# Last FFN product transposed and in one-pass format, causal mask in tiles of 32 rows, in a planned attention and FFN kernel

## Chip, core and metric

The kernel runs on one core of a Trainium2 chip. The metric is the device time of one execution in microseconds, the median of several runs. All of the work is one launch: inputs come from HBM, the activations stay on chip through all four layers, and the result goes back to HBM.

## What is computed

The input x has 16 sequences of 256 tokens with 128 features. Four residual layers follow each other, each on a layer-normalized input: attention a (2 heads of 64, part of each head rotated), an FFN, attention b (16 heads of 8 with a causal mask), and the same FFN with the same weights once more.

```python
x = x + attn_a(layernorm(x))
x = x + ffn(layernorm(x))
x = x + attn_b(layernorm(x))
x = x + ffn(layernorm(x))

def ffn(x):                                  # tlin(x, w, s) = (x @ w.T) * s
    h = silu(tlin(x, w1_w, w1_s)) * tlin(x, w2_w, w2_s)       # 128 -> 512
    h = gelu(tlin(h, h1_w, h1_s), approximate=False)          # 512 -> 512
    h = gelu(tlin(h, h2_w, h2_s), approximate=False)          # 512 -> 512
    return tlin(h, w3_w, w3_s)                                # 512 -> 128

# attn_b: the mask hides query positions before the key; softmax over the keys
scores = where(arange(n)[:, None] <= arange(n)[None, :], scores, -10000.0)
```

The FFN's weights hold only -1, 0 and 1; their scales stand in vectors of their own.

## The kernel before

**Tiles.** The 4,096 tokens are cut into eight batches (`NP`) of 512 tokens (`TOK`), that is two sequences. The residual of batch i stays in the SBUF tile `XR[i]`. An FFN works on transposed activations, features on the partitions and 512 tokens along the row. There are 16 FFN passes, eight with the tag `f` after attention a and eight with the tag `g` at the end.

**The planner.** The kernel's operations are not issued as they are written. Each is recorded as an `Op` with an engine, a cost in us written by hand, and a rank. `Plan.laid` then lays them out on a modelled clock, always taking on each engine one that could begin first (`WEIGH` says how much a change of table or of matmul mode counts there), and among near equals the one with the lowest value of `order_of`, from the table `ORDER` with a start and a step per batch for every stage. Each tile of a `Group` takes one of its buffers, and an operation can't be laid before one is free. The result is a fixed order on each engine. An operation given by `either` goes to whichever of two or three engines the planner takes. Every recorded instruction has the line 291 in the profile, so groups are told apart by tiles: `w` is a PSUM bank or a shared work buffer, `s` the four-bank score buffer, of which there is one (`g_scores`), `h` a hidden layer, `u` a Gelu or Silu output.

**The FFN.** The full-precision matmuls of this kernel run as two instructions each in the trace. Most FFN products avoid them: `parts` rounds an activation to the one-pass format as `hi` and keeps the remainder as `lo`, and `product` multiplies both halves with weights that are exact in that format. At the start a check on ACT (`low`) sums the bits that rounding would lose; where there are any, a second branch of the program runs, which is not run here. The first layer's two products have 128 features in, the two hidden ones 512. A hidden layer takes two buffers of `g_h` (hi and lo), of which there are four, handed out in turn. The second Gelu writes a full-precision tile of its own (`g_h2`, called `hl` in the profile; other tiles called `hl` in the code stand in shared buffers called `w`). The last product is full precision and not transposed: for each of four blocks of 128 tokens, the activation is the stationary side and `w3_sb`, 128 wide and multiplied by its scale beforehand, the moving one:

```python
        for t in range(TB):
            pe = p("PE", 0.87, "1")
            for c in range(NC):
                pe.matmul(
                    py[:, t * E : (t + 1) * E],
                    lhsT=h[:, c, t * P : (t + 1) * P],
                    rhs=w3_sb[:, c, :],
                    start=(c == 0),
                    stop=(c == NC - 1),
                )
```

The result already has tokens on the partitions, and DVE adds it to `XR[i]`.

**Attention b.** For each of 16 sequences the kernel goes twice through all scores, in four groups of four heads. First `attention_b_max` forms them with queries on the partitions: eight matmuls that each use 32 rows of the array, four at a time in its four row groups. Four matmuls of all 128 rows then add the mask, a diagonal `eye` times a tile `hide` of zeros and -3e38, and a reduction on DVE takes the maxima. Then `attention_b` forms the scores again with keys on the partitions, with the maxima subtracted by row-packed matmuls with `pick`; ACT takes the exponential and POOL clears the masked part. Both go through the one buffer `s`.

Of the kernel before, what the change touches and what calls it, by code (L numbers as in the profile page):

```python
# [11 lines left out]
F32 = mybir.dt.float32  # L12
F32R = mybir.dt.float32r
# [81 lines left out]
class Plan:  # L95
# [5 lines left out]
    WEIGH = {"ACT": 1.54, "PE": 0.00}  # L101
# [67 lines left out]
    def laid(self):  # L169
# [28 lines left out]
        for _ in range(len(self.ops)):  # L198
            best = None
            for e, ops in ready.items():  # L200
# [23 lines left out]
                if not cands:  # L224
# [5 lines left out]
                    (x for x in cands if x[0] + weigh * x[1] <= first + 0.012),  # L230
# [63 lines left out]
class _Recorder:  # L294
# [19 lines left out]
P = 128  # L314
# [27 lines left out]
    (INPUT, "a"): (-781, 18.6),  # L342
    (MAIN, "a"): (-863, 52.3),
    (NORM, "f"): (377, 0),
    (FILL, "f"): (88, 87.2),
    (INPUT, "b"): (299, 73.8),
    (MAXIMA, "b"): (-1830, 180.0),
    (MAIN, "b"): (448, 22.6),
    (NORM, "g"): (827, 180.7),
    (FILL, "g"): (423, 113.4),  # L350
}
LATER_AT = -505
# [17 lines left out]
R_BQKV, R_BO, R_OB, R_W3S, R_FREQ, R_END = 0, 384, 512, 640, 768, 769  # L370

C_BQ, C_BK, C_BV, C_W1S, C_W2S, C_H1S, C_H2S, C_END = 0, 1, 2, 3, 7, 11, 15, 19
# [3 lines left out]
def hybrid_kernel(ctx: ExitStack, tc: tile.TileContext, x, rows, cols, wa, wb, w12, h1, h2, w3, out):  # L376
# [28 lines left out]
    g_u, g_h, g_h2 = group("u", 4), group("h", 4, True), group("hl", 1)  # L405
# [15 lines left out]
    w3_sb = fixed([P, NC, E], "w3_sb")  # L421
# [16 lines left out]

    w12v, h1v, h2v = w12, h1.rearrange("(c p) o -> p c o", p=P), h2.rearrange("(c p) o -> p c o", p=P)
# [3 lines left out]
    for dst, src, lag in ((w12_sb, w12v, 8.0), (h1_sb, h1v, 10.0), (h2_sb, h2v, 14.0)):  # L443
        rounded.append(load("POOL", lag, dst, src, "weights"))
        exact.append(p.tile(work, [P, src.shape[1], DH], F32, f"w{len(exact)}", g_32 if exact else g_16))
# [5 lines left out]
    load("SP", 16.0, w3_sb, w3.rearrange("(c p) o -> p c o", p=P), "loads")  # L451
# [52 lines left out]
    for t in range(2):  # L504
# [13 lines left out]


# [7 lines left out]
    hide = fixed([P, 2 * P], "hide", BF16)  # L527
    o = p("POOL", 0.8)
    o.memset(hide[:], 0.0)
    o.affine_select(  # L530
        out=hide[:].rearrange("p (b k) -> p b k", b=2),
        in_=hide[:].rearrange("p (b k) -> p b k", b=2),
        compare_op=ALU.is_ge,
        fill=-HUGE,
        base=0,
        pattern=[[0, 2], [-1, P]],
        channel_multiplier=1,
    )
    eye = fixed([P, P], "eye", BF16)
    p("POOL", 0.3).tensor_copy(eye[:], ident[:])  # L540
# [48 lines left out]
    for c in range(NC):  # L589
        p("POOL", 0.45).tensor_tensor(w3_sb[:, c, :], w3_sb[:, c, :], rows_sb[:, R_W3S : R_W3S + E], ALU.mult)  # L590
# [13 lines left out]
    for n, w in enumerate(exact):  # L604
        k = w.tile.shape[1] * DH
        bits = w[:].rearrange("p c o -> p (c o)").bitcast(U16).rearrange("p (n b) -> p n b", b=2)[:, :, 0]
        p("ACT", 0.25 + 0.82e-3 * k).activation(
            p.tile(work, [P, 2048], mybir.dt.bfloat16, f"junk{n}", g_24)[:, 0:k], bits, AF.Copy, accum_out=low[:, n : n + 1]
        )
# [24 lines left out]

    def sb(shape, name, g, quota=None, dtype=F32):
        return p.tile(work, shape, dtype, name, g, quota)
# [11 lines left out]
    def layernorm_T(i, what, bias=None):  # L648
# [20 lines left out]
        for t in range(TB):  # L669
            by, mean = rstd[:, t : t + 1], mv[:, t, 0:1]  # L670
            p.either(
                ("DVE", 0.26, "tensor_scalar", (xh[:, t, :], XR[i][:, t, :], mean, by, ALU.subtract, ALU.mult), {}),
                ("ACT", 0.24, "activation", (xh[:, t, :], XR[i][:, t, :], AF.Identity), {"bias": shift[:, t : t + 1], "scale": by}),
            )
# [129 lines left out]
    def attention_b_inputs(i):  # L804
# [3 lines left out]
        for name, c0, bias in (("q", 0, C_BQ), ("k", P, C_BK)):  # L808
# [5 lines left out]
                ("ACT", 0.67, "activation", (hl[:, 0, :], pp[:], AF.Identity), {"bias": plus}),  # L814
                ("DVE", 0.72, "tensor_scalar", (hl[:, 0, :], pp[:], plus, None, ALU.add), {}),
            )
            p("DVE", 0.77).scalar_tensor_tensor(hl[:, 1, :], pp[:], plus, hl[:, 0, :], ALU.add, ALU.subtract)
# [24 lines left out]
    def attention_b_max(i, s, q0, k0, q1, k1, v):  # L842
# [10 lines left out]
        for g in range(4):  # L853
# [3 lines left out]
            o = p("PE", 0.28 + 0.15 + 0.42, ("4r", "1"))  # L857
# [12 lines left out]
            for a in range(4):  # L870
                o.matmul(sc[:, a, P : 3 * P], lhsT=eye[:], rhs=hide[:], start=False, stop=True, skip_group_check=True)
# [181 lines left out]
    def ffn(i, what):  # L1053
# [35 lines left out]
        for layer, (w_sb, wv, cs) in enumerate(((h1_sb, h1v, C_H1S), (h2_sb, h2v, C_H2S))):  # L1089
            h_in = h  # L1090
            h = sb([P, NC, TOK], f"h2_{n}", g_h2) if layer else hidden(1)
            phs = [bank(f"ph{layer}_{n}_{o}") for o in range(NC)]
            us = [h[:, o, :] if layer else sb([P, TOK], f"t_{n}_{o}", g_u)[:] for o in range(NC)]
            ps = [
                product(ph, w_sb, wv, slice(o * P, (o + 1) * P), *h_in, NC, [u] + ([] if layer else h), part_of=o)
# [7 lines left out]
            for o, (ph, u) in enumerate(zip(phs, us)):  # L1103
                if o > 1:
                    ps[o](0, 2 * NC)
                p("ACT", 0.59, "gelu", rank=(FIRST, what, i, 0)).activation(u, ph[:], AF.Gelu, scale=cols_sb[:, cs + o : cs + o + 1])
                if not layer:
                    parts(h, o, u)
        py = bank(f"pf_{n}")
        for t in range(TB):  # L1110
            pe = p("PE", 0.87, "1")
            for c in range(NC):
                pe.matmul(
                    py[:, t * E : (t + 1) * E],
                    lhsT=h[:, c, t * P : (t + 1) * P],
                    rhs=w3_sb[:, c, :],
                    start=(c == 0),
                    stop=(c == NC - 1),
                )
# [5 lines left out]
    g_m3 = group("m3", 2)  # L1125

# [73 lines left out]
```

## Time and profile before

| | |
|---|---|
| median of 3 runs | 787.37 us (785.58 to 787.78) |
| the profiled execution | 785.15 us |
| its span | 783.4 us |
| first and last score matmul of attention b | 187.4 and 712.8 us |
| granted TensorE clock, mean | 0.984 |
| table loads on ACT | 103, 132.1 us |

Busy time is the time in which an engine worked on an instruction; a matmul's record lasts from its start to the end of its pipeline, so records of matmuls overlap, and the busy time of a group is the union of its records. In the rows of groups the columns are the busy time of all, the mean of one in ns, and after the second bar the idle time of the engine in front of them with what ended it. In the chain's rows and the timeline's, the first number is the start and the second the duration, in us.

### The profile page before, as it was taken

The numbers are of one execution on the slowest core, as the hardware profiler recorded it, in microseconds if no ns is written. First come the engines' busy times: TensorE is split into PE (matmuls) and PEld (weight loads), VectorE is DVE, ScalarE is ACT, GpSimd is POOL, SyncE is SP. The second block draws the span as 40 slices with busy tenths as digits, with TensorE's granted clock in tenths as the row PEclk, the third lists the DMA queues.
The fourth block names the chain that finished last, engine by engine and source line by source line (L and its number), as shares of the span: only waits on it lengthen the run. The fifth ranks groups of instructions, "written<-read, shape, count | busy, mean of one in ns | idle before, by whom it ended". The sixth has DMA issues, their size and how long they took to land.

```text
span 783.4 us, 14329 instructions
## 1 busy us (share of the span) xinstructions
PE 718.8 (92%) x5700; PEld 510.5 (65%) x5700; DVE 499.7 (64%) x1051; ACT 529.7 (68%) x790; POOL 269.5 (34%) x422
## 2 busy tenths in 40 slices
PE   4796899988999999999999999899998989999996
PEld 2564566767677775775675768576665765756775
DVE  6887896485864866656666674856666467463641
ACT  4566777774689759776657675765768566689652
POOL 8765554042406315144325422313324233131000
PEclk9798999999999999999999999999999999999999
DMA  8400000006004225043052110404322022000000
GB/s 295 143 1 1 1 1 1 1 25 191 1 33 129 54 109 162 1 133 84 2 161 54 33 24 1 123 1 121 97 79 56 1 69 55 2 14 2 14 15 18
DMA packets 37789, 45.20 MB, mean 58 GB/s; under 512 B 1744, under 2 KB 26832, under 8 KB 37712
## 3 DMA queue, kind: packets, MB, share of 16 engines
q0 software_dynamic: 18096, 19.40, 10.2%
q1 hardware_dynamic: 19328, 24.39, 8.9%
q8 instruction: 46, 0.75, 0.4%
q10 hardware_dynamic: 288, 0.39, 0.2%
q14 instruction: 31, 0.25, 0.1%
HBM read 25.31 MB, written 18.87 MB: 56 GB/s over the span
## 4 chain that ended last, share of the span: by engine, by line
PE 64%; DVE 16%; ACT 10%; issue 4%; POOL 3%; DMA 2%; SPq 0%; POOLq 0%; DVEq 0%; ACTq 0%
PE w L291 53%; PE s L291 11%; ACT L291 3%; ACT w L291 3%; DVE u L291 2%; DVE small L291 2%; DVE h L291 2%; DVE w L291 2%; DVE m L291 2%; ACT u L291 2%; POOL w L291 1%; DVE x L291 1%; DMA x<-in_x 1%; ACT hl L291 1%; POOL rope L291 1%
## 5 line engine op out<-in xcount | busy, mean ns | idle before, releaser
L291 PE MATMUL w<-h,h_sb 128*128 128x512 f32 x1024 | 278.2, 411 | 6.2 <-DVE h L291 1.9
L291 PEld LDWEIGHTS w<-h,h_sb 128*128 128x128 f32 x1024 | 182.2, 189 | 58.2 <-issue 5.4
L291 ACT ACTIVATE u<-w,cols_sb 128x512 f32<-128x512 f32 x128 | 87.3, 687 | 76.3 <-PE w L291 75.5
L291 ACT ACT_TABLE_LOAD x103 | 132.1, 1283 | 9.5 <-DVE small L291 4.8
L291 POOL TENSOR_SCALAR_AFFINE_SELECT w<-w 128x1024 f32<-128x1024 f32 x64 | 71.7, 1120 | 192.3 <-ACT w L291 187.8
L291 DVE TENSOR_REDUCE m<-s 128x12 f32<-128x1536 f32 x64 | 112.3, 1754 | 25.2 <-PE s L291 24.6
L291 ACT ACTIVATE w<-s 128x1536 f32<-128x1536 f32 x64 | 92.9, 1451 | 25.7 <-PE s L291 20.9
L291 DVE TENSOR_TENSOR h<-u,h 128x512 fp32r<-128x512 f32 x102 | 72.7, 713 | 31.0 <-ACT h L291 28.7
L291 PE MATMUL s<-qk,qk 32*128 32x256 f32 x1024 | 73.3, 331 | 7.3 <-ACT w L291 3.6
L291 PEld LDWEIGHTS s<-qk,qk 32*128 32x128 f32 x1024 | 44.5, 184 | 47.4 <-issue 15.1
L291 DVE SCALAR_TENSOR_TENSOR u<-w,cols_sb,u 128x512 f32<-128x512 f32 x64 | 47.6, 744 | 38.6 <-ACT u L291 38.6
L291 ACT ACTIVATE hl<-w,cols_sb 128x512 f32<-128x512 f32 x64 | 41.7, 687 | 37.7 <-PE w L291 37.5
L291 PE MATMUL w<-w_sb,hl 128*128 128x128 f32 x512 | 62.1, 276 | 0.5 <-ACT hl L291 0.3
L291 PE MATMUL w<-xTffn,w_sb 128*128 128x512 f32 x128 | 57.4, 448 | 4.2 <-ACT u L291 1.8
L291 PEld LDWEIGHTS w<-w_sb,hl 128*128 128x128 f32 x512 | 59.6, 192 | 2.1 <-ACT hl L291 1.2
L291 PE MATMUL w<-w,vp 128*32 128x256 f32 (+1 forms) x1024 | 54.3, 331 | 3.6 <-POOL w L291 2.5
L291 POOL TENSOR_TENSOR h<-u,h 128x512 fp32r<-128x512 f32 x26 | 33.4, 1289 | 63.0 <-ACT h L291 51.7
L291 PE MATMUL w<-xlffn,w_sb 128*128 128x512 f32 x128 | 52.8, 413 | 1.6 <-DVE xlffn L291 1.6
L291 DVE TENSOR_TENSOR x<-w,x 128x512 f32<-128x512 f32 (+1 forms) x40 | 23.1, 579 | 47.8 <-PE w L291 47.7
L291 PEld LDWEIGHTS w<-w,vp 128*32 128x32 f32 x1024 | 27.1, 109 | 31.4 <-issue 11.1
L291 ACT CAST h<-u 128x512 fp32r<-128x512 f32 x66 | 40.9, 620 | 4.3 <-DVE u L291 2.3
L291 ACT ACTIVATE w<-s,small 128x256 f32<-128x256 f32 x64 | 29.5, 478 | 16.1 <-DVE small L291 12.7
(156 smaller groups left out, 1080.5 us busy)
## 6 DMA issues: line engine op xcount, KB each, us to landing
far_q<-w SPq DMA_DIRECT2D x16, 512.0 KB, 3.0
far_k<-w SPq DMA_DIRECT2D x16, 512.0 KB, 3.7
qk<-far_q POOLq DMA_DIRECT2D x16, 512.0 KB, 4.3
qk<-far_k POOLq DMA_DIRECT2D x16, 512.0 KB, 5.0
w<-in_h SPq DMA_DIRECT2D x2, 1024.0 KB, 11.2
h_sb<-in_h POOLq DMA_DIRECT2D x2, 1024.0 KB, 10.6
out<-x SPq DMA_DIRECT2D x8, 256.0 KB, 2.4
x<-in_x SPq DMA_DIRECT2D x7, 256.0 KB, 9.2
```

Source lines behind the costliest of these rows:

```text
L291: getattr(getattr(self.nc, self.ENGINES[op.engine]), name)(*a, **k)
```

## The change

**The FFN's last product.** The second Gelu's output is cut into halves like the first's, in two more buffers of `g_h` (`g_h2` is gone). `w3_sb` becomes a rounded tile with a check of its own at the start, without the scale. The product is formed transposed, by eight one-pass matmuls of 512 tokens with the weight as the stationary side. ACT or DVE takes it out of PSUM with the scale, which is now a column per output feature; four transposes bring the tokens back to the partitions, and DVE adds the result to `XR[i]` as before.

**The mask.** `eye` and `hide` become four slices each, one for each 32 columns of the diagonal. 16 matmuls of 32 rows take the place of four of 128 rows, four at a time in the array's row groups like the scores. Slice sl covers columns 32·sl to 127 of two blocks: 256, 192, 128 and 64 columns. The tiles are made at the start by two iotas on POOL and five instructions on DVE.

**The planner.** Costs, `WEIGH`, the tolerance and all entries of `ORDER` have other values, so the order on every engine differs.

```diff
-    WEIGH = {"ACT": 1.54, "PE": 0.00}
+    WEIGH = {"ACT": 0.55, "PE": 0.23}
-                    (x for x in cands if x[0] + weigh * x[1] <= first + 0.012),
+                    (x for x in cands if x[0] + weigh * x[1] <= first + 0.097),
 ORDER = {
-    (INPUT, "a"): (-781, 18.6),
-    (MAIN, "a"): (-863, 52.3),
...
+    (INPUT, "a"): (-751, 23.1),
+    (MAIN, "a"): (-700, 21.5),
...
-LATER_AT = -505
+LATER_AT = -849
-    g_u, g_h, g_h2 = group("u", 4), group("h", 4, True), group("hl", 1)
+    g_u, g_h = group("u", 4), group("h", 4, True)
-    w3_sb = fixed([P, NC, E], "w3_sb")
+    w3_sb = fixed([P, NC, E], "w3_sb", F32R)
-    for dst, src, lag in ((w12_sb, w12v, 8.0), (h1_sb, h1v, 10.0), (h2_sb, h2v, 14.0)):
+    for dst, src, lag in ((w12_sb, w12v, 8.0), (h1_sb, h1v, 10.0), (h2_sb, h2v, 14.0), (w3_sb, w3v, 15.0)):
-    load("SP", 16.0, w3_sb, w3.rearrange("(c p) o -> p c o", p=P), "loads")
+    load("SP", 16.0, exact[3], w3v, "loads")
+    skew = sb([P, 4, P], "skew", g_16, None, I32)
+    p("POOL", 0.7).iota(skew[:], pattern=[[-32, 4], [1, P]], base=0, channel_multiplier=0)
...
+    o = p("DVE", 0.7)
+    o.tensor_scalar(rowi[:], rowi[:], 31, None, ALU.bitwise_and)
+    o.tensor_copy(row[:], rowi[:])
+    o.tensor_copy(away[:], skew[:])
...
+    o.tensor_scalar(eye[:], away[:], row[:, 0:1], None, ALU.is_equal)
+    o.tensor_scalar(hide[:], away[:], row[:, 0:1], -HUGE, ALU.is_gt, ALU.mult)
-    for c in range(NC):
-        p("POOL", 0.45).tensor_tensor(w3_sb[:, c, :], w3_sb[:, c, :], rows_sb[:, R_W3S : R_W3S + E], ALU.mult)
-            o = p("PE", 0.28 + 0.15 + 0.42, ("4r", "1"))
+            o = p("PE", 0.55, "4r")
-            for a in range(4):
-                o.matmul(sc[:, a, P : 3 * P], lhsT=eye[:], rhs=hide[:], start=False, stop=True, skip_group_check=True)
+            for sl in range(4):
+                for a in range(4):
+                    rows = slice(32 * a, 32 * a + 32)
+                    o.matmul(
+                        sc[:, a, P : 3 * P].rearrange("p (b k) -> p b k", b=2)[:, :, 32 * sl : P],
+                        lhsT=eye[rows, sl, :],
+                        rhs=hide[rows, sl, 32 * sl : P].unsqueeze(1).to_broadcast([32, 2, P - 32 * sl]),
+                        start=False,
+                        stop=sl == 3,
+                        skip_group_check=True,
+                    )
-            h = sb([P, NC, TOK], f"h2_{n}", g_h2) if layer else hidden(1)
+            h = hidden(1 + layer)
-                if not layer:
-                    parts(h, o, u)
-        py = bank(f"pf_{n}")
-        for t in range(TB):
...
+                parts(h, o, u)
+        yT = sb([P, TOK], f"yT_{n}", g_yT)
+        pf = bank(f"pf_{n}")
+        product(pf, w3_sb, w3v, slice(0, E), *h, NC, [yT])
+        by = cols_sb[:, C_W3S : C_W3S + 1]
+        p.either(
+            ("ACT", 0.53, "activation", (yT[:], pf[:], AF.Copy), {"scale": by}),
+            ("DVE", 0.61, "tensor_scalar", (yT[:], pf[:], by, None, ALU.mult), {}),
+        )
+        py = bank(f"py_{n}")
+        o = p("PE", 0.38, "1")
         for t in range(TB):
+            o.transpose(py[:, t * E : (t + 1) * E], yT[:, t * P : (t + 1) * P], ident[:])
```

## Prediction

> **What bounds the kernel now.** I read the page's totals, slices and chain first, then the groups by shape, then the PE timeline of a dense stretch, then the chain at the end. Totals, slices and chain:
>
> ```profile
> PE 718.8 (92%) x5700; PEld 510.5 (65%) x5700; DVE 499.7 (64%) x1051; ACT 529.7 (68%) x790; POOL 269.5 (34%) x422
> PE   4796899988999999999999999899998989999996
> PE 64%; DVE 16%; ACT 10%; issue 4%; POOL 3%; DMA 2%; SPq 0%; POOLq 0%; DVEq 0%; ACTq 0%
> ```
>
> From the fifth slice on PE is at least 80% busy, mostly 90%, and it holds 64% of the chain. DVE and ACT hold 26% of it with two thirds of the span busy: they still have room, but their latency is felt. The groups that the change touches or resembles (busy us, mean ns of one):
>
> ```profile
> L291 PE MATMUL w<-h,h_sb 128*128 128x512 f32 x1024 | 278.2, 411 | 6.2 <-DVE h L291 1.9 <-DVE u L291 1.5 <-ACT u L291 1.4
> L291 PE MATMUL w<-w_sb,hl 128*128 128x128 f32 x512 | 62.1, 276 | 0.5 <-ACT hl L291 0.3
> L291 PE MATMUL s<-hide,eye 128*128 128x256 bf16 x256 | 39.5, 277 | 0.0
> L291 PE MATMUL s<-mT,pick 32*128 32x256 f32 x512 | 33.6, 277 | 0.0
> L291 PE MATMUL w<-ident,oT 128*128 128x128 f32 x64 | 10.0, 279 | 0.1
> L291 DVE TENSOR_REDUCE m<-s 128x12 f32<-128x1536 f32 x64 | 112.3, 1754 | 25.2 <-PE s L291 24.6
> L291 DVE TENSOR_TENSOR h<-u,h 128x512 fp32r<-128x512 f32 x102 | 72.7, 713 | 31.0 <-ACT h L291 28.7
> L291 ACT CAST h<-u 128x512 fp32r<-128x512 f32 x66 | 40.9, 620 | 4.3 <-DVE u L291 2.3
> L291 POOL TENSOR_TENSOR h<-u,h 128x512 fp32r<-128x512 f32 x26 | 33.4, 1289 | 63.0 <-ACT h L291 51.7 <-DVE h L291 11.3
> L291 ACT ACT_TABLE_LOAD x103 | 132.1, 1283 | 9.5 <-DVE small L291 4.8 <-PEq L1191 1.3 <-PE s L291 1.0
> ```
>
> The first row is the one-pass format that the last product moves to; the second is the last product now, 32 records per FFN because each of its 16 full-precision matmuls runs as two. The stretch of attention b, 187 to 713 us, looks like this on PE:
>
> ```profile
> 205.50 0.51 PE L291 MATMUL s<-qk,qk 32*128 32x256 f32 x8
> 205.94 0.61 PE L291 MATMUL s<-hide,eye 128*128 128x256 bf16 x4
> 206.31 2.58 PE L291 MATMUL w<-h,h_sb 128*128 128x512 f32 x10
> 208.82 0.51 PE L291 MATMUL s<-qk,qk 32*128 32x256 f32 x8
> ```
>
> A period of 3.32 us is scores, mask and ten FFN matmuls back to back, with no idle: there PE is the limit, and the reduce (1.754 us) that frees the one score buffer is hidden behind the ten. From 187 to 713 us PE is busy 500.7 of 526 us, DVE 335.2, ACT 369.5. But the score buffer is nearly as full: work on it takes 115.8 us on PE, 112.3 on DVE and 91.4 on ACT, 319.5 of the 526, and the rest is some 128 hand-overs of 1.6 us each. So two resources are close together here, PE and the chain through the score buffer.
>
> **The last product, on PE.** By the rows, 32 x 0.121 = 3.88 us per FFN go, and 8 x 0.272 = 2.17 us and four transposes of 0.156 (row of oT) = 0.63 us come: -1.08 us. By the start-to-start times in the trace's records (0.112, 0.234, 0.109) it is 3.58 against 1.87 + 0.44, -1.27 us. I take -1.2, as these matmuls stand in streams: 16 FFNs give **-19.2 us** (-17.3 to -20.3). In the first stage (two of them) PE is also 93% busy from 140 us on, so I count all alike.
>
> The row of oT has a transpose at 0.156 us of PE's busy time. The Trainium skill (TensorE: Matmul & The Clock Gate, Part 4) puts one at about 275 ns in a kernel's context, which speaks against the change; by that the 64 new ones would cost 17.6 us, an estimate from that page, and the saving would fall by some 8 us. The streams of four here end sooner, and I keep the row.
>
> **The mask, on PE.** Now four matmuls of 256 columns, 0.109 to 0.120 us from start to start, after 0.207 us in which the row-packed scores drain; with the change of mode behind them, 0.65 us. The new form has 16 of 32 rows, four at a time, over 256, 192, 128 and 64 columns, with no change of mode in front. No row shows these widths; the nearest are the row-packed groups of 256 columns:
>
> ```profile
> 227.14 0.39 PE L291 MATMUL s<-qk,qk 32*128 32x256 f32 x4
> 227.37 0.29 PE L291 MATMUL s<-mT,pick 32*128 32x256 f32 x4
> 227.49 0.28 PE L291 MATMUL s<-qk,qk 32*128 32x256 f32 x4
> 227.60 0.28 PE L291 MATMUL s<-mT,pick 32*128 32x256 f32 x4
> ```
>
> Four of them cost one step of 0.11 to 0.12 us. Upper bound: narrow steps cost as much, 4 x 0.116 + 0.205 us to leave the mode = 0.67 us (+0.02). Lower bound: steps shrink with the columns, 0.116 + 0.109 + 0.082 + 0.055 + 0.124 = 0.49 us (-0.16). I take -0.10, between them: 64 groups give **-6.4 us** (-10.2 to +1.3). The busy time of the pick row, 33.6 / 512 = 0.066 us each, would make 16 of them 1.05 us against 39.5 / 64 = 0.62, so +27.8 us; it holds the drain of every short burst, so I leave it to the rivals. The reduce also starts earlier, by 0.1 to 0.2 us.
>
> The Trainium skill (the same page, "Wait — 56ns, not 53.3ns?") has matmuls start no closer than about 25 ns however narrow. The records of the four packed scores start 2 to 4 ns apart, so here the trace disagrees; by the rule 16 would need 0.40 us, an estimate, inside my bounds.
>
> **What it adds elsewhere.** The built programs give the counts: subtractions 102 to 145 on DVE and 26 to 47 on POOL; rounding copies 66 to 127 on ACT, 62 to 63 on DVE, 0 to 2 on POOL; 16 scaled evictions (11 DVE at 0.747, 5 ACT at 0.69); 22 normalizations moved from ACT to DVE; table loads 103 to 108. On ACT that is +37.8 +3.5 +6.4 and, with the moved work, about +34 us; on DVE +30.7 +8.2 +10 and small ones, about +56; on POOL +27. ACT and DVE end near 72%. Eleven of 16 FFNs lie in the attention-b stretch: some +38 us on DVE and +23 on ACT there, on queues that also hold the reduces and exponentials. Their share on the chain now (DVE 16% of 783 = 125 of 500 us busy, ACT 78 of 530) would put 38 x 0.25 + 23 x 0.15 = 13 us on the path. The lower bound is nothing, as PE has FFN matmuls of other batches to do. I take half, **+6.5 us**.
>
> **The order.** The hidden tiles now serve three layers from the same four buffers, so an FFN's first layer waits for its predecessor's second product. On PE, in the last two FFN pairs, the last product now stands directly behind the second hidden one; before, five first-layer matmuls (1.2 us) lay between. Its last two matmuls need Gelu 0.70, copy 0.5 and subtraction 0.69 us with their hops, about 2.1 us, behind six matmuls of 1.4 us: 0.7 us of PE idle, and first-layer matmuls are queued behind. Two or three times: **+1.8 us**. Everything else on PE is the same work reordered: behind the last exponentials stand 172 hidden matmuls instead of 136, 8.4 us that attention b no longer has to carry, counted once on each side.
>
> **The end.** The chain there now:
>
> ```profile
> 772.77 0.70 ACT hl L291
> 773.51 3.18 PE w L291 x26
> 777.13 0.69 DVE x L291
> ```
>
> From the last Gelu's start to the add, 4.36 us. Then: Gelu 0.70, copy 0.5, subtraction 0.69, two matmuls 0.62, eviction 0.72, transposes 0.60 and hops 0.9: 4.75. **+0.4 us**.
>
> **The start.** The mask's tiles are made by five DVE instructions, in the queue ahead of the first statistics (now at 4.03 us), and wait for a 512-wide iota on POOL. The nearest rows are integer casts of 0.39 to 0.88 us and POOL's 256-wide memset of 0.31; the statistics could be up to 2 us late, of which DVE's wait for the second input (2.33 us) absorbs part. The rounding load of w3 on POOL's queue (0.8 us of issue, by the same loads of the other weights) and its check on ACT ahead of the fork (some 0.6 us: 1.04 for 1,024 columns, 1.89 for 2,048) replace four scalings of 0.456 on POOL. **+1 us** (0 to 2.5).
>
> **Sum.** -19.2 - 6.4 + 6.5 + 1.8 + 0.4 + 1.0 = -15.9 us. The profiled execution took 785.15 us (span 783.4); the median of the runs is 787.37, 2.2 higher. On the median: 771.5 us.
>
> **Rivals.** *The score buffer's chain takes over (slower).* Place: 187 to 713 us, 128 hand-overs. If each waits d longer behind the new copies and subtractions, while PE's saving turns idle, the stretch changes by 128d less 64 x 0.15 us for the earlier end of the mask; with -2 for the first stage and +6.6 at the end (the 8.4 us of hidden matmuls moved there, -3.6 for three last products, +1.8) the sum is 128d - 5. It is slower from d = 0.04 us. If a third of the 61 us added there falls ahead of readers, d = 0.16 us: +15.5, **803 us**. For it: the buffer's near full use. Against: the 3.32 us periods wait for PE, not for the reduce.
> *The narrow mask steps cost as much as the pick row's busy time.* +27.8 instead of -6.4: **806 us**. Against: the four lines of steps above.
> *The gain is just given back.* Full 13 us on the path, the mask at its upper bound, the last product at -17.3, start +2.5, other terms as above: +1.7 us; or a tie within 2.4 us, **787 us**.
> *It does not do what it says.* The built program has 128 matmuls of 512 columns, 64 transposes and 1,024 mask matmuls; ruled out.
>
> **Numbers.** The forecast has 0.72, with its own range from all good ends (-20.3 - 10.2 and nothing given back or lost, 757) to nearly none (785). The score chain 0.14, the mask 0.06, the tie 0.08. The range runs 756 to 791: below it is little, above it most of the two slower rivals. A difference under 0.3% (2.4 us) can't be told from none. Faster 0.72, same 0.08, slower 0.20.
>
> **What would show it.** In the profile after: PE's busy time near 695 us; groups of 16 mask matmuls that end 0.8 to 0.95 us after the first score matmul; periods of scores and eight FFN matmuls near 2.8 us; the reduce's and exponential's idle time little changed. The score chain shows as PE idle over 60 us between 187 and 700 us with waits of PE for the reduce or the exponential. I am wrong if PE's busy time falls by over 20 us and the span doesn't, or if the new last product's busy time is over 45 us with its transposes.

## The result and the profile after

The changed kernel takes 807.54 us (median of 4 runs, 806.07 to 814.14), the kernel before 786.80 us in the same call: 1.0283 times as long, with a 95% interval of 1.0251 to 1.0315. The prediction was 771.5 us. The profiled execution of the changed kernel took 806.07 us, its span is 804.2 us. The page's totals, PE's and the clock's slices and the chain of the changed kernel:

```profile
PE 712.6 (89%) x6148; PEld 488.1 (61%) x6148; DVE 558.2 (69%) x1138; ACT 564.4 (70%) x836; POOL 297.7 (37%) x441
...
PE   3788889988898889987998989999989999999886
...
PEclk9799899999999999988999999999999999999998
...
PE 51%; DVE 23%; ACT 11%; issue 5%; POOL 5%; DMA 4%; SPq 0%; DVEq 0%; POOLq 0%; ACTq 0%
```

PE did lose work, but only 6.2 us of busy time (718.8 before), and its share of the chain went from 64 to 51%. The slices say where it now stands still: from the fifth to the nineteenth, mostly nines before, nine of fifteen are now eights and one is a seven. The span adds up over PE's records: the first matmul starts 1.65 us later (8.45 before, 10.10 now), busy time is 6.2 us less, the gaps between the records are 26.1 us more (49.4 and 75.5), and what follows the last one is 0.7 us less. Together +20.8 us, the whole difference of the spans.

The groups that the prediction priced, in the changed kernel (busy us, mean ns of one, then idle time in front):

```profile
L291 PE MATMUL w<-h,h_sb 128*128 128x512 f32 x1024 | 281.5, 414 | 9.9 <-DVE h L291 5.5 <-ACT u L291 1.2 <-DVE mT L291 1.2
...
L291 DVE TENSOR_TENSOR h<-u,h 128x512 fp32r<-128x512 f32 x145 | 103.7, 716 | 77.5 <-ACT h L291 75.1
...
L291 ACT CAST h<-u 128x512 fp32r<-128x512 f32 x127 | 78.8, 620 | 4.0
...
L291 PE MATMUL w<-h,w_sb 128*128 128x512 f32 x128 | 38.6, 416 | 1.0 <-DVE h L291 0.5
...
L291 PE MATMUL s<-hide,eye 32*128 32x256 bf16 x256 | 18.5, 278 | 0.0
...
L291 PE MATMUL s<-hide,eye 32*128 32x192 bf16 x256 | 16.2, 241 | 0.0
...
L291 PE MATMUL s<-hide,eye 32*128 32x128 bf16 x256 | 14.4, 214 | 0.0
...
L291 PE MATMUL s<-hide,eye 32*128 32x64 bf16 x256 | 12.7, 188 | 0.0
...
L291 PE MATMUL w<-ident,yT 128*128 128x128 f32 x64 | 10.2, 282 | 0.9 <-ACT yT L291 0.8
```

The last product (`h,w_sb`) with its transposes (`ident,yT`) is 48.8 us of busy time instead of 62.1; subtractions and copies are as many as counted. The four rows of mask steps overlap and must not be added; one group with its end is read from the timeline, where the first number is the start in the span and the second the time to the end of the last:

```profile
212.42 0.51 PE L291 MATMUL s<-qk,qk 32*128 32x256 f32 x8
212.76 0.45 PE L291 MATMUL s<-hide,eye 32*128 32x256 bf16 x16
```

Scores and mask together end 212.76 + 0.45 - 212.42 = 0.79 us after the first score matmul; in the period that the prediction shows of before it was 205.94 + 0.61 - 205.50 = 1.05 us. (The unrounded records give 0.80 us for this group and for every one of the 64.) So both pieces of new work do on PE about what they were meant to do. What changed for the worse is when PE gets to them. The waits of PE in attention b (187 to 700 us), the longest four in the changed kernel (what was waited for, us in total, times, longest):

```profile
PE w L291 <- POOL w L291: 7.3, 9, 2.3
PE s L291 <- DVE m L291: 6.0, 11, 1.3
PE s L291 <- ACT w L291: 5.2, 9, 1.2
PE w L291 <- ACT u L291: 3.6, 7, 0.8
```

The same view of the kernel before has for the first three of them:

```profile
...
PE s L291 <- ACT w L291: 3.4, 6, 1.2
...
PE w L291 <- POOL w L291: 2.5, 4, 1.3
PE s L291 <- DVE m L291: 1.8, 4, 0.7
```

The new waits are for the causal clearing on POOL, the maxima on DVE and the exponentials on ACT: steps of attention b that the change doesn't touch. Busy time in this stretch went from 487.9 to 473.6 us of 513, so PE has 14.3 us more of idle there, and the stages moved: first score matmul of attention b 187.4 to 200.9 us, last one 712.8 to 724.5 us, end of the span behind it 70.6 to 79.7 us.

### The profile page after: what moved, and what is told of

It reads as the page before. It is cut to its first block, busy times and chain, and to the rows that moved or that the text cites. A ratio compares the mean times of both kernels' runs of the same rounds, so it can differ in the third digit from the quotient of the medians.

```text
span 804.2 us, 15414 instructions
## 1 busy us (share of the span) xinstructions
PE 712.6 (89%) x6148; PEld 488.1 (61%) x6148; DVE 558.2 (69%) x1138; ACT 564.4 (70%) x836; POOL 297.7 (37%) x441
## 4 chain that ended last, share of the span: by engine, by line
PE 51%; DVE 23%; ACT 11%; issue 5%; POOL 5%; DMA 4%; SPq 0%; DVEq 0%; POOLq 0%; ACTq 0%
PE w L291 42%; PE s L291 9%; DVE m L291 4%; DVE w L291 4%; ACT w L291 4%; ACT L291 3%; DVE h L291 3%; DVE small L291 3%; DVE u L291 2%; ACT u L291 2%; DMA qk<-far_k 1%; POOL w L291 1%; DMA x<-in_x 1%; DVE x L291 1%; DMA far_q<-w 1%
## 5 line engine op out<-in xcount | busy, mean ns | idle before, releaser
L291 PE MATMUL w<-h,h_sb 128*128 128x512 f32 x1024 | 281.5, 414 | 9.9 <-DVE h L291 5.5
L291 PEld LDWEIGHTS w<-h,h_sb 128*128 128x128 f32 x1024 | 185.5, 192 | 64.0 <-DVE h L291 9.8
L291 ACT ACTIVATE u<-w,cols_sb 128x512 f32<-128x512 f32 x192 | 129.8, 686 | 106.4 <-PE w L291 101.9
L291 DVE TENSOR_TENSOR h<-u,h 128x512 fp32r<-128x512 f32 x145 | 103.7, 716 | 77.5 <-ACT h L291 75.1
L291 POOL TENSOR_TENSOR h<-u,h 128x512 fp32r<-128x512 f32 x47 | 60.3, 1285 | 125.8 <-ACT h L291 108.9
L291 ACT ACTIVATE w<-s 128x1536 f32<-128x1536 f32 x64 | 92.8, 1450 | 19.9 <-PE s L291 19.2
L291 ACT CAST h<-u 128x512 fp32r<-128x512 f32 x127 | 78.8, 620 | 4.0
L291 PE MATMUL w<-ident,w 128*128 128x128 f32 x192 | 33.2, 313 | 12.4 <-DVE w L291 8.5
L291 PE MATMUL w<-h,w_sb 128*128 128x512 f32 x128 | 38.6, 416 | 1.0 <-DVE h L291 0.5
L291 PEld LDWEIGHTS w<-xTffn,w_sb 128*128 128x128 f32 x128 | 24.6, 192 | 24.2 <-ACT u L291 8.0
L291 PEld LDWEIGHTS w<-ident,w 128*128 128x128 f32 x192 | 24.9, 158 | 23.4 <-DVE w L291 8.9
```

Of the source, the lines that this page charges most:

```text
L291: getattr(getattr(self.nc, self.ENGINES[op.engine]), name)(*a, **k)
```

## Experiments

Seven theories were tried; the letters are those of the expectations. **A**: the halves of the second layer load ACT, DVE and POOL and hold up the score buffer's readers. **B**: the planner's new values lay a worse order, whatever the work. **C**: the order before was an unusually good fit to exactly the old work, and whatever makes the planner lay again loses that. **D**: the chain that now holds the last product in the order of recording, and the shared buffers, take the room to run ahead (a chain is a row of operations that must begin in the order in which they were recorded). **E**: the clock, which falls behind waits of PE, costs the difference. **F**: the new work needs a worse order only because of its own waits, in front of the transposes and for the shared buffers. **G**: in the new order the FFN's steps lie too thinly between the score groups.

### One part at a time, laid by the planner

Four kernels hold a part of the change each: the mask; the last product with its halves; the planner's new values and costs; both pieces of work without the new values. In each the planner lays the order anew.

```diff
 mask_only: the kernel before, with
-            o = p("PE", 0.28 + 0.15 + 0.42, ("4r", "1"))
+            o = p("PE", 0.55, "4r")
...
 ffn_only: the kernel before, with
-            h = sb([P, NC, TOK], f"h2_{n}", g_h2) if layer else hidden(1)
+            h = hidden(1 + layer)
...
 order_only: the kernel before, with
-    WEIGH = {"ACT": 1.54, "PE": 0.00}
+    WEIGH = {"ACT": 0.55, "PE": 0.23}
...
 both_old_order: the changed kernel, with
-    WEIGH = {"ACT": 0.55, "PE": 0.23}
+    WEIGH = {"ACT": 1.54, "PE": 0.00}
...
```

> The kernel before with the new mask alone (its tiles, its 16 row-packed matmuls, and their cost of 0.55 us in the plan); the last FFN product and the planner's values stay as before. Theory A (the halves that the new last product adds on ACT, DVE and POOL hold up the score buffer's readers) expects the mask's own saving: 777 to 787 us. Theory B (the planner's new values lay a worse order, whatever the work) expects the same 777 to 787 us. Theory C (any edit moves the planner off an order that had been fitted to exactly the old work) expects a loss here too: 790 to 805 us. The late first statistics on DVE, if they come from the mask's tiles, should put PE's first matmul near 10 us here.

> The kernel before with the new last FFN product alone (halves, one-pass product, scaled eviction, four transposes, four hidden buffers for three layers); the mask and the planner's values stay as before. Theory A expects 800 to 815 us, with PE idle more than before between the scores. Theory B expects 770 to 785 us, the PE saving of some 17 us less what is given back. Theory C expects a loss of 5 to 20 us: 792 to 807 us.

> The kernel before with the planner's new values alone (weights, tolerance, the table of ranks, and the changed costs of operations that both kernels have); no work is changed. Theory A expects 780 to 795 us. Theory B expects 800 to 815 us, with the first score matmul near 200 us instead of 187. Theory C expects a loss as well, 795 to 815 us, and can't be told from B by this run alone.

> The changed kernel's work (new mask and new last product) with the old planner values. Theory A expects 800 to 812 us, like the changed kernel. Theory B expects 765 to 782 us. Theory C expects 795 to 815 us, as the old values do not fit the new work.

Measured: mask alone 817.2 us (ratio 1.0397, 1.0351 to 1.0442), last product alone 847.5 (1.0771, 1.0720 to 1.0821), new values alone 821.6 (1.0443, 1.0402 to 1.0485), new work with the old values 831.6 (1.0569, 1.0528 to 1.0611); before 785.9. Each part alone is worse than all of them together. The mask alone adds no halves and keeps the old values, and loses 31 us, which speaks against A and B; and for the new work the new values are the better ones (807.5 against 831.6), so B falls as it stands, though on the old work the new values do lose 36 us. Only C expected a loss in all four, and it had the sizes wrong: each came out above its range, by 7 us (new values) to 40 us (last product). But in these kernels work and order change together, so what follows holds the order fixed.

### The old order as a list

From here on a kernel called "fixed" doesn't call the planner's search. It carries the order of another kernel as a list, operation for operation with engine and buffer; operations that the list doesn't know go into the nearest gap.

```diff
-    order = p.laid()
-    early, late = ([o for o in order if (o.begin < p.cut) is e] for e in (True, False))
+    early, late = p.given(SEQ)
```

> The kernel before with its own planned order written out as a list, operation for operation, and only the mask step exchanged: sixteen narrow steps for one wide one in each of the 64 score groups, and the two mask tiles made on POOL and DVE later in the first stage. Nothing is left out. Theory A (the halves hold up the score buffer's readers) and theory C (any edit moves the planner off the order that was fitted to the work) both give the mask's own price, as the groups of the changed kernel show it: 64 groups that end about 0.1 us earlier, so 779 to 783 us. If the narrow steps themselves cost what the re-planned mask kernel lost (+31 us), 810 to 820 us.

Measured 781.9 us, before 787.4 in the same call: 0.9938 of it (0.9917 to 0.9959). The page's totals and PE's slices:

```profile
PE 711.9 (91%) x6468; PEld 509.4 (65%) x6468; DVE 502.5 (64%) x1056; ACT 529.4 (68%) x790; POOL 269.0 (34%) x421
...
PE   4797899989899999998998999899998989999996
```

PE's busy time fell by 6.9 us and the slices keep the nines. The mask was priced at -6.4 us and gives about -5; the same edit with the order laid anew gave +31. Some 36 us between two kernels with the same work are the order's alone (here and below, the order includes which engine and which buffer an operation takes).

The last product in the old order, in three steps: turned round without halves (the low half is left out and the high one taken twice at half scale), with the halves' work beside it, and as the changed kernel has it.

```diff
 ffn_round_fixed
-            h = hidden(1 + layer)
+            h = [sb([P, NC, TOK], f"h2_{n}", g_h2, None, F32R)] * 2 if layer else hidden(1)
-        product(pf, w3_sb, w3v, slice(0, E), *h, NC, [yT])
+        product(pf, w3_sb, w3v, slice(0, E), *h, NC, [yT], None)
...
 ffn_load_fixed: the same, and copy and subtraction for each block of the second layer
 ffn_fixed: halves in g_h, read by the product, which is in the chain
```

> The order of the kernel before as a list, the old mask, and the last product turned round with its four transposes, but without the halves: the second hidden layer's Gelu writes the rounded format by itself into the buffer it had, and the product is taken twice over that one tile, each time at half scale. It leaves out the low half of the second hidden layer. This is the change's effect on PE alone. Its busy time falls by 62.1 - 48.8 = 13.3 us by the two profiles, from start to start by about 20. Theory C: the order stands, so the span falls by 10 to 19 us, to 767 to 776 us. Theory A says the same here, since the halves are gone. If the product's new form itself does harm (its transposes wait for a reader, or it waits for the product buffer), 790 us or more.

> The one before this (order of the kernel before, product turned round, the low half left out of the product) and with it the work of the halves on ACT, DVE and POOL: the same copies and subtractions as in the changed kernel, with a remainder that no product reads. Theory A: that load delays the score buffer's readers, and the gain is lost: 790 to 810 us. Theory C: in an order that stands, the load costs what there was of room, 0 to 7 us over the kernel without it: 768 to 783 us.

> The last product as the changed kernel has it (halves in the shared buffers, both read by the product, the product in the chain that keeps all FFN products in the order of recording), with the old mask, laid by the list of the kernel before as far as the chain and the buffers let it: the next FFN's first layer, up to 22 us ahead in the kernel before, is held behind the last product. Nothing is left out. Theory A: 795 to 815 us. Theory C: near the kernel with the load, 770 to 785 us. Theory D (the chain and the shared buffers of the halves take the room to run ahead): 5 to 20 us above the kernel with the load alone.

Measured: 799.4 us (1.0146, 1.0119 to 1.0173), 803.1 (1.0223, 1.0178 to 1.0268) and 842.6 (1.0710, 1.0678 to 1.0742), before 787.4. The first is a miss for A and C both, which had 767 to 776 us: PE's busy time fell by 8.1 us, its gaps grew by 25.4, and the scores alone waited 9.7 us more. Of the 17.7 us by which its profiled span is longer, 8.6 are there before attention b begins (first score matmul at 196.0 us instead of 187.4). The second lies in the range that A gave, but only because the first is slow already: the halves' load itself costs 0.8% or some 6 us by the ratios (3.7 by the medians), give or take 4, far from the 20 that A wanted; **A falls as the main cause**. The step to chain and shared buffers costs another 39 us, where D had expected 5 to 20.

```diff
 ffn_round_late: the transposes of ffn_round_fixed, 1.5 us further back in PE's list
```

> The kernel with the product turned round in the order of before and no halves (low half left out, as before), with one difference: the four transposes stand 1.5 us further back in PE's list, so that other steps of PE lie between the last product and the transposes that wait for its eviction. PE stood still for 7.3 us in front of the transposes. If that wait is what the new form lost, 785 to 793 us instead of 799.4; if the loss is the rest of the order, which no longer fits (the scores waited 17.0 us instead of 7.3 us), 796 to 801 us.

Measured 803.4 us (1.0207, 1.0162 to 1.0252), outside both of its ranges. PE's wait in front of the transposes fell from 7.3 to 3.1 us and the time did not follow. But most of the wait only moved, to the first-layer matmuls behind. The waits of PE that ended with the eviction `yT`, in ffn_round_fixed (first two lines) and here:

```profile
PE w L305 <- ACT yT L305: 5.7, 4, 2.6
PE w L305 <- DVE yT L305: 1.1, 1, 1.1
```

```profile
PE w L305 <- ACT yT L305: 4.4, 4, 2.1
PE w L305 <- DVE yT L305: 1.1, 1, 1.1
```

So the run does not rule this wait out. It bounds it: 6.8 us of the 25.4 by which PE's gaps grew.

```diff
 chain_fixed: the kernel before in its own order, but
-            pe = p("PE", 0.87, "1")
+            pe = p("PE", 0.87, "1", chain="ffn")
```

> The work of the kernel before in its own order as a list, with one rule more: the old last product joins the chain in which the FFN's products start in the order of recording, as the changed kernel has it. The next FFN's first layer then waits for the last product of the one before, and 149 instructions move back by 0.5 to 22 us. Nothing is left out. Theory D (the chain is what takes the room): 800 to 825 us, since the changed product in the old order with chain and shared buffers took 842.6 against 803.1 us without them. If the shared buffers of the halves did that instead, 786 to 793 us.

Measured 816.5 us (1.0368, 1.0322 to 1.0415), inside D's range: one rule on the order, and no work at all, costs 31 us. Most of it falls in one place, where the first FFN of the last stage may no longer begin 22 us ahead: of the 64 score groups with a mask, the 40th is 5 us later than before, the 42nd 30 us. Windows of before and of this kernel (stretch, its length, busy time of each engine with its instructions, granted clock, DMA share, GB/s), before first:

```profile
470.00:515.00 45.00, 41.60 (x385) 30.46 (x384) 30.19 (x60) 27.60 (x32) 11.47 (x16) 0.96 0.19 54
```

```profile
470.00:515.00 45.00, 35.44 (x211) 23.68 (x209) 19.46 (x40) 19.15 (x23) 7.25 (x8) 0.77 0.00 1
```

PE goes through 211 instructions where it went through 385, at a clock of 0.77. So **D holds for the old order**: the chain forbids moves that this order is built on.

### The new order as a list

The other half of the crossing: the order of the changed kernel, kept, and its work taken back piece by piece.

```diff
 after_oldmask_fixed: the changed kernel and its order, with
-            o = p("PE", 0.55, "4r")
+            o = p("PE", 0.28 + 0.15 + 0.42, ("4r", "1"))
...
 after_nohalves_fixed: the changed kernel and its order, with one buffer less for each third layer and
-            us = [sb([P, TOK], f"t{layer}_{n}_{o}", g_u) for o in range(NC)]
+            us = [h[0][:, o, :] if layer else sb([P, TOK], f"t_{n}_{o}", g_u)[:] for o in range(NC)]
...
-                parts(h, o, u)
+                if not layer:
+                    parts(h, o, u)
...
-        product(pf, w3_sb, w3v, slice(0, E), *h, NC, [yT])
+        product(pf, w3_sb, w3v, slice(0, E), h[0], h[0], NC, [yT])
 oldwork_after_order: the kernel before, with the list SEQ of the changed one
```

> The changed kernel in its own exact order, written out as a list, with the wide mask step of before put back in every score group. Nothing is left out. The mask's worth in this order, by the difference to the changed kernel: in the order of before it was 787.4 - 781.9 = 5.5 us, so 811 to 815 us by theory C (the order) and by theory A (the halves). If the narrow steps do harm in this order, under 805 us.

> The changed kernel in its own exact order without the halves of the second hidden layer: 64 copies and 64 subtractions fewer on ACT, DVE and POOL; Gelu writes the rounded format by itself, and the last product is taken twice over that tile at half scale. It leaves out the low half of the second hidden layer. Theory A: the load of the halves is what the changed kernel loses, so 785 to 792 us. Theory C: in the order of before the same load cost 803.1 - 799.4 = 3.7 us, so 801 to 806 us here.

> The work of the kernel before (wide mask, four-pass last product, no halves behind the second layer) in the exact order of the changed kernel. Nothing is left out. Theory C: the order itself loses, so the old work in it is as slow as the changed kernel or slower by what the change takes off PE: 805 to 830 us. Theory F (the new work needs a worse order only because of its own waits, the transposes behind an eviction and the halves in shared buffers): with those gone the old work runs in this order near its old time, 785 to 797 us.

Measured: 809.6 us (1.0311, 1.0261 to 1.0361), 801.6 (1.0200, 1.0151 to 1.0248) and 829.0 (1.0571, 1.0515 to 1.0626), before 785.9. The last one settles it: **the new order costs the old work some 43 us**, and with the order held the new work gains it 22 of those back. F falls with it (it had 785 to 797 us). The 43 us may hold some misfit, as this list was laid for the new work; the planner's own orders for the old work with the new values (+36) and for the new mask (+31 instead of -5) have no such part. The old mask's 809.6 us is just under the 811 to 815 that were expected, within its interval. The page of the old work in the new order:

```profile
PE 737.6 (89%) x5700; PEld 516.9 (63%) x5700; DVE 513.1 (62%) x1068; ACT 522.9 (63%) x766; POOL 284.8 (34%) x434
...
PE   3887799989989989978989899898999999999996
```

These are the same 5,700 matmuls as in the kernel before, and PE is busy 18.8 us longer over them (47.8 us of the span are at half clock instead of 23.9, which accounts for up to 12 us) and idle 24.0 us longer between them. The eights are there without any new work. Against this page the changed kernel's 712.6 us of PE is 25.0 less: what the prediction had summed for the two edits, -25.6. The new order with the old mask stands between them:

```profile
PE 718.7 (89%) x5380; PEld 486.9 (60%) x5380; DVE 555.6 (69%) x1133; ACT 564.5 (70%) x836; POOL 297.1 (37%) x442
```

So the last product takes 18.9 us off PE and the mask 6.1, where 19.2 and 6.4 were put.

Theory G came from the FFN's hidden steps in the dense stretch. The windows of the steps on `h` (PE's busy time and count come first), in the kernel before and then in the old work in the new order:

```profile
260.00:390.00 130.00, 50.62 (x182) 31.93 (x182) 15.08 (x25) 8.16 (x14) 8.96 (x7) 1.00 0.24 74
```

```profile
260.00:390.00 130.00, 36.18 (x124) 22.31 (x124) 11.19 (x17) 5.57 (x9) 10.24 (x8) 0.97 0.23 66
```

### The new work in other orders

```diff
 after_refit_1, _2, _3: the changed kernel with other planner values, here _2
-    WEIGH = {"ACT": 0.55, "PE": 0.23}
+    WEIGH = {"ACT": 1.79, "PE": 0.04}
-    (NORM, "f"): (759, 7.8),
-    (FILL, "f"): (264, 112.0),
+    (NORM, "f"): (841.5, 7.7),
+    (FILL, "f"): (162.9, 114.5),
...
```

> Exactly the work of the changed kernel, laid by the same planner with a third set of its values (ranks and weights of the kinds of work; the diff has no other line). Nothing is left out. Theory C: the time follows the order and not the work, so the same work in another order comes out at least 8 us away from 807.5: 780 to 799 us if this order is a lucky one, above 815 if not. Theory G (in the changed kernel the FFN's steps lie too thinly between the score groups: by the profiles 124 hidden steps between 260 and 390 us with the old work in the new order, 182 in the order of before): the time falls with the share of FFN steps in that stretch. If the new work itself is the cause, 804 to 811 us.

> As the one before, with a fourth set of the planner's values, in which the score groups' ranks and the weights differ most from the changed kernel's. Same expectations: 780 to 799 or above 815 us by theory C, 804 to 811 us if the new work itself is the cause.

> The work of the changed kernel, unchanged, with a fifth set of the planner's values, reached from the set that gave 788.7 us by small steps. Nothing is left out. Theory C: the time follows the order; the work itself is 13 to 21 us lighter than before's, so an order as good as the one before had would take 766 to 775 us, and one near the 788.7 us order 780 to 792 us. If the new work can't be laid as well as the old one, because of its chain and its shared buffers, it stays at 785 us or above.

Measured: 802.4 us (1.0185, 1.0136 to 1.0234), 788.7 (1.0035, 1.0014 to 1.0056) and 786.0 (0.9985, 0.9964 to 1.0007). The first lies in none of the ranges that were given for it. With 807.5 and 831.6 us from above, the same new work takes 786 to 832 us in five orders. **The second half of C is shown**: the 20.7 us of loss belong to the order that was laid, not to the work. Its first half goes too far, as the old order fits the new mask as well (781.9 us). But none of the five brings the work's 25 us of PE into the span; the third is level with before. Whether the new work allows a better order is open: no run lays it without its chain or with more buffers, and 785 us or above was what the third run's expectation gave if these keep good orders away. The page of the second:

```profile
PE 705.9 (90%) x6148; PEld 484.0 (62%) x6148; DVE 555.1 (71%) x1130; ACT 574.7 (73%) x845; POOL 303.3 (39%) x446
...
PE   3788999899898999999798988999999999998986
```

G falls as a rule. The hidden steps in 260 to 390 us (without the new last product, which reads `h` too) are 182 in the kernel before and 126 in the changed one, but 192 and 156 in the orders of 802.4 and 788.7 us, and 182 again in the old work with the new values, at 821.6 us: the time doesn't follow them.

### The clock

```diff
+            if op.index in WARM:
+                keep = ("matmul", (dst,), dict(lhsT=self.zero[:, 0:P], rhs=self.zero[:, P:wide], start=fresh, stop=False, ...))
+                op.calls[:0] = [keep] * WARM[op.index]
```

> The changed kernel in its own order, with idle steps for PE in eleven places: ahead of instructions that PE waited 0.9 to 3 us for, four to eighteen short matmuls of zeros by zeros go into the bank that the waiting instruction will write. They add nothing to any result. Theory E (the clock): the changed kernel spends 51.2 us at half clock where the kernel before spends 23.9, each stretch behind a wait of PE of about 1.2 us or more; (51.2 - 23.9) / 2 = 13.7 us of the 20.7 lost would be this. Filling the waits takes most of those stretches away and leaves the waits themselves: 793 to 801 us, half-clock time under 30 us. If PE is not what decides in those stretches, 805 to 809 us, with the half-clock time gone all the same.

> The new mask in the order of before (781.9 us), with idle steps for PE ahead of 13 instructions that it waited 0.9 to 4.2 us for, as in the changed kernel's run: short matmuls of zeros into the bank that is written next. Nothing is left out. Theory E (the clock): its half-clock stretches of 23.9 us lie mostly in the first 75 us and lose 10.9 us; with half of them gone 776 to 780 us. If the clock follows something else than the single waits, 781 to 784 us.

Measured: 805.3 us (1.0247, 1.0206 to 1.0288) against 807.5 without, and 781.5 us (0.9922, 0.9892 to 0.9952) against 781.9. The idle steps do what they should where they stand. The same 6.7 us of the changed kernel, which follow a wait of 2.3 us for POOL, without them and with them (PE's busy time first, the clock third from the end):

```profile
349.10:355.80 6.70, 6.51 (x58) 3.66 (x62) 3.60 (x13) 2.21 (x3) 3.85 (x8) 0.50 0.66 152
```

```profile
349.10:355.80 6.70, 6.61 (x98) 4.61 (x94) 4.28 (x13) 5.55 (x9) 5.87 (x9) 1.00 0.82 250
```

In the whole changed kernel seven of its eleven half-clock stretches went and five others came, 51.2 us before and 44.4 after; under 30 had been expected, so here the test stayed half done. In the order of before it is cleaner: 23.9 us fell to 10.2, which would be 6.8 us of time if a stretch at half clock loses half its length, and the time fell by 0.4 us, which can't be told from nothing. **E falls** as the main cause: the time hardly follows the clock's dips. (Whether the idle steps cost some time of their own was not measured.)

## Why the prediction was wrong

**The step that failed** is the part on the order. It put +1.8 us, from two places where the last product now stands in front of a first layer, and called everything else on PE "the same work reordered". The old work in the new order shows +43 us for that reordering, and the planner's own new order of the old work +36. The paragraph did see the rule that holds the next first layer behind the last product, but priced it by two or three short waits; in the old order the same rule costs 31 us. How much of the 43 us it makes in the new order no run shows. The 172 against 136 hidden matmuls behind the last exponentials were rightly read (the tail grew by 9.1 us for 8.4 counted), but "8.4 us that attention b no longer has to carry" did not come back: from first to last score matmul attention b took 525.4 us before and 523.6 now, and PE's idle time from 187 to 700 us grew by 14.3 us. The first stage, for which the prediction had no term but the start, ends 13.5 us later; the old work in the new order has 10.4 of these.

**The last product** was priced at -19.2 us on PE and +6.5 for the halves, -12.7. With the new order held its work on PE is 18.9 us less and the halves cost some 6 us, in both orders and give or take 4: the two terms held. The time went from 829.0 to 809.6 us, -19.4, which is 7 us more than their sum; that list was laid for the new product, and no run tells how much of this is its fit. A bound did not hold: the product with its transposes was to stay under 45 us of busy time and is 48.8. The one-pass steps are 38.6 / 128 = 0.302 us of busy time each, not 0.272, so the row of the long hidden streams was too low for groups of eight; the transposes, 0.159 us against 0.156, were right. No order showed the product's gain against the kernel before, though, and in that kernel's own order the turned product lost 12 us even without halves. Waits for its eviction hold 6.8 of the 25.4 us by which PE's gaps grew there; the rest is open.

**The mask** was priced at -6.4 us; it gives 5 in the old order and 2 in the new one, where the ratios leave it anywhere from a loss of some 3 to a gain of 7. A group ends 0.80 us after the first score matmul, at the lower edge of the 0.8 to 0.95 foreseen. (The 0.40 us that the prediction works out for 16 steps lies below its bounds of 0.49 to 0.67, not inside them; nothing rests on it.)

**Start and end.** The start cost 1.65 us where 1.0 was put. At the end, from the last Gelu to the add, 4.75 us were foreseen; the timeline has 794.18 to 798.27, 4.09:

```profile
794.18 0.69 ACT L291 ACTIVATE u<-w,cols_sb 128x512 f32<-128x512 f32 x1 [0.25 <-PE w L291]
796.83 0.69 ACT L291 ACTIVATE yT<-w,cols_sb 128x512 f32<-128x512 f32 x1 [1.31 <-PE w L291]
798.27 0.69 DVE L291 TENSOR_TENSOR x<-w,x 128x512 f32<-128x512 f32 x1 [2.02 <-PE w L291]
```

**The rivals.** The chain through the score buffer had 803 us and 14 in 100, near the time and not the cause: its sign was to be over 60 us of PE idle between 187 and 700 us, and there are 39.4, of which the reduce and the exponential hold 11.2; and its mechanism, the halves, costs 6 us. The narrow mask steps at the pick row's busy time are ruled out by the mask in the old order. No rival named the order. Of the two signs of error that the text set itself, the busy time of the last product is met (48.8 us). The other, "PE's busy time falls by over 20 us and the span doesn't", is not: against the kernel before PE's busy time fell by 6.2 us only, because the order had put 18.8 us of busy time and 24.0 us of idle on top, and at equal order it fell by 25.0 us and the time by 22. The text had no sign for a loss by the order.

**How it could have been priced.** The kernel before has 49.4 us of gaps on PE in all. Of the changed kernel and the eighteen run here only one has fewer, the mask in that same order with idle steps that fill gaps (46.2; 53.7 without them); the newly laid orders have 62 to 97. A list with so little slack is itself a part of the speed. Wherever the change made the planner lay again, the fair term, in hindsight, was a loss of unknown size, from nothing to the 31 to 43 us that the study shows, and the chance of "faster" perhaps no better than even.

## What to carry to other kernels

When an order is searched for, the order is a tuned part: an edit that makes the search run again changes two things, and the second can be several times the first. Before judging such an edit, hold the order as a list and exchange only the work; then lay several orders of the new work and compare the best of each side. Here this found that the mask alone, in the old order, is worth keeping (781.9 us, 0.6% under before), and that the last product is not, at least in the orders tried.

A rule on order that looks free, one chain more, may cost as much as any work: it showed 31 us for no instruction added.

## What was not expected of the hardware

The granted clock fell to half, for 3.4 us or a multiple, behind short waits of PE: in the changed kernel behind 2.30 us at 347 us, behind 1.35 us at 777 us, at 550 us even where the longest waits of the 9 us ahead were 0.75 and 0.52 us, and in the kernel before behind one of 1.19 us at 415 us, while one of 1.34 us at 697 us left it alone. So the "about 1.2 us or more" of the expectation doesn't hold for every stretch, and no threshold comes out of these runs. In such a stretch a group of 16 small matmuls takes 1.51 us instead of 0.86:

```profile
343.34 0.86 PE L291 MATMUL w<-w,vp 128*32 128x256 f32 x16
349.29 1.51 PE L291 MATMUL w<-w,vp 128*32 128x256 f32 x16 [2.30 <-POOL w L291]
```

Matmuls of zeros, issued into the wait, kept the clock at 1.00 there, but the whole kernel's time fell by only 2.2 us, less than its interval.

The narrow mask steps shrink with their width even when four run side by side: in the records of the group at 212.42 us the next four start 0.120 us behind 256 columns, 0.083 behind 192 and 0.056 behind 128, close to the lower bound of the prediction (0.109, 0.082, 0.055).
